# Adding own terms by accumulating DMAs in a two-branch adaLN block on one Trainium2 core

## The chip, the cores and the metric

The kernel runs on one core of one Trainium2 chip. The time is the device time of one execution in microseconds. TensorE (PE) multiplies matrices, VectorE (DVE), ScalarE (ACT) and GpSimd (POOL) work element by element on 128 partitions, SyncE (SP) issues DMAs. Each engine takes its instructions strictly in order and waits on semaphores for the others. A DMA issued by POOL can add to its destination instead of overwriting it.

## The reference

Four batches of 256 tokens by 256 channels go through two residual steps. Both start from the same two-sided weighted sum over the tokens, with `k = v = side` and decay `d` per batch and channel:

```python
ek = exp(min(k, 30)); ekv = ek * v
a = a * decay + ekv_t        # forward and reversed: nf, nb; the same for ek: df, db
euk = exp(min(u + k, 30))
num = nf + nb - ekv + euk * v
den = df + db - ek + euk
out = sigmoid(r) * num / max(den, 1e-8) * (0.8 + 0.2 * tf)
```

Branch 1 (weights w1, u1) feeds a gated recurrence: two 256 x 256 matmuls, `alpha = exp(-8 softplus(lambda) sigmoid(.))`, `beta = sqrt(1 - alpha^2 + 1e-6)`, and a linear scan over tokens; its result is added to x. Branch 2 (w2, u2), gated by the new x, feeds a mixture of experts: two shared experts for all tokens and the top 2 of 8 routed ones (hidden size 640). All is float32.

## The kernel before, in words

Channels lie on partitions, in two halves; a batch is a 128 x (2, 256) tile, and den and num stand side by side as four quarters (two of den, two of num). The work of a batch b is `front(b)` and `shared_units(b)`:

- `exps(b)`: POOL writes min(k, 30) (L432) and min(u + k, 30) (L437, four halves a batch) into `ek` and `own`, ACT takes the exponentials (L453, L460), DVE multiplies by v (L456, L464).
- `sums(b, n)` for branch n: a scan forward (L486, four quarters), its scaled last column (L492), and a scan backward over the forward sums (L499). The two-sided sum is (1 - d^2) times the backward scan (`rev`), plus the own term. Batch 0 (`BY_PE`) adds both on PE by matmuls with the identity and with a diagonal of 1 - d^2 (L513). Batches 1 to 3 add on DVE, two operations a branch (L521), each with the factor `both` = 1 - d^2, into the tile `fwd`.
- `most` takes the maximum with 1e-8 (batch 0 on ACT, L536; the others on DVE, L533). `quotient` takes 1/den as exp(-log) on ACT (L552 to L555), and three DVE operations make the gated product (L557/559, L560, L562).
- `gates` multiplies by x (L577), runs eight matmul steps on PE (L584), and then tanh, exponential, square and square root on ACT (L592 to L619) with two DVE steps (L598, L618). `recurrence` is L625, two scans (L628), the sum into x (L634), a tanh (L635) and the product `xt` (L637).
- `token_rows(b)` makes router scores and token-major rows on PE (L708, L715). `shared_units(b)` runs the shared experts: 40 matmul steps (L804), SiLU on ACT (L810), a product on DVE (L812), 20 matmul steps (L780). The 40 identity matmuls of `keep_warm` (L642) fill PE in batch 0.
- After the last front come `route`, `places` and `divide` (many small DVE operations), the scatter of token rows to DRAM (POOL, L974), loads of expert weights and rows (SP), and 18 slots of routed experts (L1065, L1081), each ended by an accumulating scatter into the output (L1095).

Natural logarithm, square root, SiLU and tanh need different ACT tables; a table load is L178. The DRAM rows are first blanked: POOL makes four empty rows (L683), and SP writes each out (L1318), which the scatter waits for.

The order is written out by hand: `ORDER` lists for each engine the numbers of the steps, which `Plan.run` emits in that order. Lengths and delays given with each step only merge the lists; they don't hold the chip to anything. A step that waits therefore holds all later steps of its engine.

Side and x of three batches are loaded at the start; batch 3 reuses the buffers of batch 0. The `own` and `ek` buffers alternate: batches 1 and 3 share one set, 0 and 2 the other.

Of the kernel before, what the change touches and what calls it, by code (L numbers as in the profile page):

```python
# [12 lines left out]
ALU = mybir.AluOpType  # L13
# [44 lines left out]

E30 = 10686474581524.463
# [8 lines left out]
        122 123 135 124 13 125 14 126 15 127 16 128 17 129 18 130 19 131 26 72 20 97 21 98 79 80 73 81 99 82 100 83  # L68
        75 84 85 101 132 86 133 87 88 118 134 119 136 120 137 150 197 102 138 77 103 145 104 173 201 174 105 169 163
        202 106 176 178 177 179 175 203 181 196 204 198 147 200 205 199 207 206 299 220 209 213 208 223 214 224 186  # L70
        225 215 238 305 311 192 317 210 217 325 149 212 216 211 219 218 251 392 226 380 233 379 257 261 381 262 391
        264 382 333 266 265 267 263 341 349 269 357 384 385 386 383 387 365 235 393 388 390 389 403 396 553 554 406
        555 407 280 408 274 421 237 397 474 398 480 492 394 416 418 395 400 399 401 434 402 557 409 486 559 558 556
        560 444 440 500 508 562 564 447 445 448 449 450 446 524 452 532 561 563 565 577 516 571 570 580 457 581 463
        572 582 617 584 618 566 765 567 540 620 771 621 574 568 420 569 597 573 576 575 619 583 622 623 603 624 631
        607 625 626 608 627 632 628 610 629 630 612 777 611 613 637 609 643 633 615 634 644 647 638 791 646 783 799
        670 664 639 641 642 673 674 640 676 677 675 678 645 679 683 680 684 681 682 807 696 697 689 698 685 699 700
        701 704 690 702 691 703 705 693 706 720 707 708 722 709 721 711 710 723 712 725 713 724 714 726 715 727 686
        815 728 694 716 729 730 731 717 695 718 692 719 732 736 823 852 831 858 737 870 738 739 878 864 886 894 902
        733 734 910 918 735  # L80
    """,
    "act": """
        71 24 22 25 23 74 78 76 115 116 117 144 121 171 172 155 164 156 167 166 165 168 161 162 170 195 180 148 146
        298 221 222 232 304 187 310 193 316 324 244 243 253 252 249 250 255 254 259 256 260 258 332 348 340 356 415
        268 234 364 236 378 419 404 405 375 275 417 479 374 485 473 491 281 427 426 436 435 432 433 438 437 439 442
        443 507 499 441 523 531 451 515 552 578 579 464 458 616 764 539 770 589 590 598 595 596 599 600 601 549 550
        602 605 606 604 776 790 614 782 798 806 672 665 822 814 671 851 830 857 840 863 869 841 877 885 901 893 909
        917 928 927
    """,
    "pe": """  # L90
        89 27 28 29 30 31 90 91 92 32 107 93 108 33 34 35 109 36 110 94 37 95 96 38 39 40 151 152 153 154 41 157 158
        111 42 159 43 44 160 45 46 47 48 49 112 50 51 52 53 54 113 55 56 57 58 114 59 60 61 62 63 64 65 66 290 292
        293 291 294 295 306 307 296 182 300 301 188 297 302 303 189 312 183 190 313 320 191 308 321 184 185 322 318
        319 323 309 314 315 239 240 241 242 245 246 247 352 248 353 326 336 344 345 328 327 337 354 338 346 355 335
        334 329 330 347 339 331 342 350 343 351 358 359 360 361 362 363 367 366 368 270 276 369 277 481 475 271 482
        272 469 371 373 487 483 278 484 488 370 273 470 372 476 477 279 471 467 489 478 490 472 422 423 424 428 429
        425 465 503 504 430 468 431 519 505 494 495 520 466 496 521 497 493 501 502 498 511 510 506 509 512 517 513
        527 522 528 529 530 525 533 518 526 514 535 536 534 537 766 459 453 460 454 767 768 461 455 462 772 456 760
        541 542 538 769 543 761 762 763 545 585 586 587 591 588 592 593 594 778 786 547 544 546 548 773 794 787 774
        788 779 795 775 789 758 756 757 784 759 796 780 792 781 797 785 635 793 636 802 803 804 800 801 805 660 666  # L100
        661 667 662 663 668 669 808 818 816 819 810 826 820 811 687 688 824 847 848 812 809 821 817 849 832 813 827
        825 850 833 835 828 829 853 834 836 859 860 861 838 854 873 855 856 865 866 874 881 837 882 862 843 867 868
        844 839 875 876 845 871 883 846 897 872 889 884 879 887 898 890 905 880 891 913 899 888 914 896 892 895 904
        903 915 900 906 907 912 908 920 911 916 919 921 922 924 926 923 925
    """,
    "pool": """
        67 68 69 70 142 143 139 140 227 141 288 230 228 231 410 411 413 229 284 286 412 282 414 658 659 657 652 648
        651 655 656 649 654 743 653 741 742 740 650
    """,
    "sp": """  # L110
        194 283 285 287 289 377 376 551 744 745 842 746 747 749 750 751 748 752 753 754 755 929
# [77 lines left out]
def adaln_attn_ffn(ctx: ExitStack, tc, xT, sideT, cond, par, wio, wr, wall, out):  # L189
# [11 lines left out]
    def fixed(name, *shape, dtype=F32):  # L201
        return const.tile([P, *shape], dtype, name=name)
# [72 lines left out]

    out_tf = fixed("out_tf", B)
# [80 lines left out]
    def tiny_step(emit, reads, writes):  # L357
        dve(2, emit, reads, writes, 11)

    def factors():  # L360
# [17 lines left out]
        tiny_step(lambda: nc.vector.reciprocal(onward, both), ["both"], ["onward"])  # L378
        tiny_step(
            lambda: nc.vector.scalar_tensor_tensor(onward, onward, -1.0, decays, ALU.mult, ALU.mult), ["decay", "onward"], ["onward"]  # L380
        )
        tiny_step(lambda: nc.vector.tensor_scalar(both, both, -1.0, None, ALU.mult), ["both"], ["both"])
        for n in (1, 2):
            for c in range(NC):
                act(
                    P, lambda n=n, c=c: nc.scalar.activation(
                        weigh[n][:, c, :], ident, AF.Copy, scale=both[:, n - 1, c, 0:1]
                    ),
                    ["both"], [("act", ACTS - n)], 11,
                )  # L390
        tiny_step(lambda: nc.vector.tensor_scalar(out_tf, tf, -0.1, -0.4, ALU.mult, ALU.add), ["tf"], ["out_tf"])

    def softplus():
# [9 lines left out]
        one(lambda: nc.vector.tensor_scalar(ser, s2, 1.0 / 17.0, None, ALU.mult), ["s2"], ["ser"])  # L403
        for k in (15, 13, 11, 9, 7, 5, 3):
            one(
                lambda k=k: nc.vector.scalar_tensor_tensor(ser, ser, 1.0 / k, s2, ALU.add, ALU.mult),
                ["ser", "s2"], ["ser"],
            )
# [8 lines left out]
    begun = []  # L417
# [7 lines left out]
    def exps(b):  # L425
# [7 lines left out]
        for n, j in ((1, U1), (2, U2)):  # L433
            d = own[n][k]
            for c in range(NC):
                pool(
                    lambda d=d, c=c, j=j: nc.gpsimd.tensor_scalar(  # L437
                        d[:, c, :], v[:, c, :], par_sb[:, j, c : c + 1], 30.0, ALU.add, ALU.min
                    ),
                    sv, [("own", n, k, 0)], r + 1, length=1450 if b == 0 else 1700,  # L440
                )
# [29 lines left out]
    def sums(b, n):  # L471
# [47 lines left out]
        for c in range(NC):  # L519
            dve(  # L520
                512, lambda c=c: nc.vector.scalar_tensor_tensor(  # L521
                    f[:, c::NC, 0:T], r[:, c::NC, 0:T], both[:, n - 1, c, b : b + 1], o[:, c::NC, :], ALU.mult, ALU.add
                ),
                [("rev", n, c), ("rev", n, NC + c), *halves("own", n, k), "both"], [("fwd", n, k, c), ("fwd", n, k, NC + c)], rank,
            )

    def most(b, n):

        k = b % 2
        den = fwd[n][k][:, 0:NC, 0:T]  # L530
        fs = [("fwd", n, k, h) for h in range(NC)]
        if (b, n) not in BY_PE:
            dve(256, lambda: nc.vector.tensor_scalar(den, den, DEN, None, ALU.max), fs, fs, 10 * b + 9)  # L533
            return
        q = bank_of(b, n)
        act(512, lambda: nc.scalar.activation(den, banks[q], AF.Relu, bias=less[:, 0:1]), [("bank", q)], fs, 10 * b + 10 + n)  # L536

    def quotient(b, n):
# [6 lines left out]
        ns = [("fwd", n, k, h) for h in range(NC, 2 * NC)]  # L545
        num, nkeys = f[:, NC:, :], ns
# [8 lines left out]
        act(512, lambda: nc.scalar.activation(y, y, AF.Exp, scale=-1.0), yk, yk, r, tables=(LOG,))  # L555
# [17 lines left out]
    def gates(b, q, qkeys):  # L573
# [4 lines left out]
        for which, dst, name in ((1, gate, "gate"), (0, xb, "xb")):  # L578
# [11 lines left out]
            for m in range(NC):  # L590
                act(
                    400, lambda m=m, which=which, dst=dst, pio=pio: nc.scalar.activation(  # L592
                        dst[:, m, :], pio[:, m, :], AF.Tanh, bias=half_b[:, which, m : m + 1], scale=0.5
                    ),
                    [("one", o), "half_b"], [(name, m)], r, tables=th,
                )
# [697 lines left out]
    def front(b):  # L1294
# [8 lines left out]
        if b + 1 < B:  # L1303
            exps(b + 1)
        gates(b, *q1)
        q2 = quotient(b, 2)
# [94 lines left out]
```

## Time and profile before

| | |
|---|---|
| median of three runs | 302.14 us (301.39 to 303.08) |
| the profiled execution's own time | 302.88 us |
| its span, first to last instruction | 300.7 us |
| busy in the span: PE, DVE, ACT, POOL | 280.6, 166.8, 125.2, 80.6 us |

The profile is one execution. A line of a group or timeline gives the source line, the engine, the operation, the tiles written and read, and how often; idle time before it is put down to what released it. "L804 PE" is the shared experts' first matmul. A matmul step in float32 shows as two records of the same line.

### The profile page before, as it was taken

To read this page: it belongs to the slowest core of one execution; us is meant where nothing else is said; L and a number is where in the kernel's file an instruction comes from. 1 tells how busy PE (TensorE), PEld (TensorE's weight loads), DVE (VectorE), ACT (ScalarE), POOL (GpSimd) and SP (SyncE) were. 2 spreads that over 40 slices of the span, in tenths; PEclk is the share of its full clock that TensorE was granted. 3 is DMA by queue.
4 is the path that set the end of the run, shared out by engine and by line. 5 is a ranking of instruction groups with operands and counts; after the bars stand their busy time and mean duration, and the time that the engine had idled before them with its cause. 6 is when DMAs were issued, how large, how long until landed. Compare 5 with 4: busy or idle time off the path is not lost. (4 is left out here: it accounts for less than half of the span.)

```text
span 300.7 us, 5206 instructions
## 1 busy us (share of the span) xinstructions
PE 280.6 (93%) x1902; PEld 247.4 (82%) x1902; DVE 166.8 (55%) x484; ACT 125.2 (42%) x250; POOL 80.6 (27%) x101
## 2 busy tenths in 40 slices
PE   7689899999999999969999999999999999999780
PEld 7579788888888888858888996899899999976770
DVE  4989999999999999860212152222322222242220
ACT  3397776997796696211212212212112111222100
POOL 6997031920000001756000002202242222124242
PEclk9799999999999999999999999999999999999995
DMA  6941000089992010269569999999269932881321
GB/s 204 442 179 35 1 3 0 0 302 353 352 348 89 0 35 2 98 216 425 183 227 430 427 415 416 408 396 401 49 170 349 326 108 35 282 280 21 39 31 22
DMA packets 22427, 60.88 MB, mean 202 GB/s; under 512 B 1920, under 2 KB 19200, under 8 KB 19840
## 3 DMA queue, kind: packets, MB, share of 16 engines
q1 hardware_dynamic: 18480, 55.02, 48.9%
q0 software_dynamic: 3360, 4.59, 8.1%
q10 hardware_dynamic: 560, 0.92, 0.9%
q8 instruction: 16, 0.26, 0.4%
q14 instruction: 11, 0.09, 0.1%
HBM read 44.60 MB, written 15.93 MB: 201 GB/s over the span
## 5 line engine op out<-in xcount | busy, mean ns | idle before, releaser
L804 PE MATMUL bank<-xt,shared 128*128 128x256 f32 x320 | 80.3, 382 | 0.8 <-DVE xt L637 0.8
L1065 PE MATMUL bank<-xg,late 128*128 128x128 f32 x640 | 75.1, 275 | 2.1 <-DVEq L1258 1.6
L1065 PEld LDWEIGHTS bank<-xg,late 128*128 128x128 f32 x640 | 73.3, 192 | 2.9 <-issue 2.3
L804 PEld LDWEIGHTS bank<-xt,shared 128*128 128x128 f32 x320 | 59.0, 190 | 9.2 <-DVE xt L637 1.3
L1072 DVE TENSOR_TENSOR act<-bank,act 128x256 f32<-128x256 f32 (+1 forms) x48 | 18.2, 380 | 70.6 <-ACT act L1071 69.2
L1095 POOL DMA_INDIRECT outT<-ys,to x16 | 24.8, 1551 | 114.5 <-DVE act L1072 40.9
L780 PE MATMUL acc<-shared,act 128*128 128x256 f32 x160 | 43.2, 382 | 2.3 <-DVE act L812 1.5
L1071 ACT ACTIVATE act<-bank 128x256 f32<-128x256 f32 (+1 forms) x48 | 16.7, 349 | 60.0 <-PE bank L1065 57.6
L1081 PE MATMUL acc<-late,act 128*128 128x256 f32 x160 | 37.7, 381 | 0.1
L780 PEld LDWEIGHTS acc<-shared,act 128*128 128x128 f32 x160 | 29.6, 190 | 7.2 <-DVE act L812 2.2
L178 ACT ACT_TABLE_LOAD x26 | 33.4, 1283 | 0.4
L974 POOL DMA_INDIRECT rows<-xtok,where x16 | 15.9, 992 | 64.1 <-DVE act L812 57.5
L1081 PEld LDWEIGHTS acc<-late,act 128*128 128x128 f32 x160 | 29.1, 190 | 4.6 <-issue 0.8
L437 POOL TENSOR_SCALAR late<-side,par_sb 128x256 f32<-128x256 f32 x16 | 26.4, 1650 | 10.9 <-DVE late L521 6.4
L810 ACT ACTIVATE act<-bank 128x256 f32<-128x256 f32 x40 | 13.9, 383 | 35.3 <-PE bank L804 35.0
L812 DVE TENSOR_TENSOR act<-bank,act 128x256 f32<-128x256 f32 x40 | 15.8, 415 | 19.7 <-ACT act L810 19.4
L486 DVE TENSOR_TENSOR_SCAN late<-decays,late 128x256 f32<-128x256 f32 x32 | 21.6, 704 | 0.0
L499 DVE TENSOR_TENSOR_SCAN late<-decays,late 128x257 f32<-128x257 f32 x32 | 21.1, 688 | 0.0
L1047 ACT COPY xg<-one 128x256 f32<-128x256 f32 x18 | 6.6, 374 | 33.6 <-PE one L1045 33.6
L584 PE MATMUL one<-late,wio_sb 128*128 128x256 f32 x64 | 15.7, 383 | 1.7 <-DVE late L577 1.7
L584 PEld LDWEIGHTS one<-late,wio_sb 128*128 128x128 f32 x64 | 11.6, 190 | 3.9 <-DVE late L577 1.7
L642 PEld LDWEIGHTS acc<-ident 128*128 128x128 f32 x80 | 11.9, 207 | 0.7
(224 smaller groups left out, 312.8 us busy)
## 6 DMA issues: line engine op xcount, KB each, us to landing
late<-in_wall SPq DMA_DIRECT2D x12, 1920.0 KB, 9.5
quad<-in_wall SPq DMA_DIRECT2D x6, 1920.0 KB, 11.2
rows<-quad SPq DMA_DIRECT2D x8, 1224.0 KB, 12.7
shared<-in_wall SPq DMA_DIRECT2D x2, 1920.0 KB, 9.0
xr<-rows SPq DMA_DIRECT2D x16, 136.0 KB, 7.9
side<-in_sideT SPq DMA_DIRECT2D x4, 256.0 KB, 4.6
outT<-base SPq DMA_DIRECT2D x4, 256.0 KB, 4.5
x<-in_xT SPq DMA_DIRECT2D x3, 256.0 KB, 9.6
```

Source lines behind the costliest of these rows:

```text
L178: line.append((free.get(engine, 0), len(line), lambda t=table: load_table(t)))
L437: lambda d=d, c=c, j=j: nc.gpsimd.tensor_scalar(d[:, c, :], v[:, c, :], par_sb[:, j, c : c + 1], 30.0, ALU.add, ALU.min),
L486: 0, lambda h=h: nc.vector.tensor_tensor_scan(f[:, h, 0:T], decay(h % NC, T), src[:, h, :], 0.0, ALU.mult, ALU.add),
L499: 0, lambda h=h: nc.vector.tensor_tensor_scan(r[:, h, 0 : T + 1][:, ::-1], decay(h % NC, T + 1), f[:, h, 0 : T + 1][:, ::-1], 0.0, ALU.mul ...
L584: 256, lambda m=m, k=k, which=which, pio=pio: nc.tensor.matmul(pio[:, m, :], wio_sb[:, which, k, bass.ts(m, P)], xc[:, k, :], start=(k == ...
L780: 256, lambda j=j: nc.tensor.matmul(acc[j], acts[a][:, bass.ts(j, P)], shared[s][:, GU + i * C : GU + (i + 1) * C], start=False, stop=((s, ...
L804: 256, lambda ps=ps, gu=gu, g=g, c=c, i=i: nc.tensor.matmul(ps[:, g, :], gu[:, g, c, bass.ts(i, P)], xt[k][:, c, :], start=(c == 0), stop= ...
L1065: nc.tensor.matmul(ps[:, g, i, :], gu[:, g, k, bass.ts(i0 + i, P)], self.xg[:, k, :], start=(k == 0), stop=(k == NC - 1),)
L1071: nc.scalar.activation(hid[:, 0:n, :], ps[:, 0, 0:n, :], AF.Silu)
L1072: nc.vector.tensor_tensor(hid[:, 0:n, :], ps[:, 1, 0:n, :], hid[:, 0:n, :], ALU.mult)
L1081: nc.tensor.matmul(self.py, self.acts[i], self.weights[:, GU + i * C : GU + (i + 1) * C], start=(i == 0), stop=(i == NI - 1),)
L1095: nc.gpsimd.indirect_dma_start(out=out[:, :], out_offset=bass.IndirectOffsetOnAxis(ap=self.to.bitcast(U32), axis=0), in_=ys, in_offset=Non ...
```

## The change

The diff, without the long number lists:

```diff
+ATANH = (0.12196954132, 0.10699280244, 0.14310103703, 0.19999355624, 0.33333339513)
...
     "pool": """
-        67 68 69 70 142 143 139 140 227 141 288 230 228 231 410 411 413 229 284 286 412 282 414 658 659 657 652 648
-        651 655 656 649 654 743 653 741 742 740 650
+        71 72 73 74 140 143 144 141 142 229 231 230 232 207 228 219 218 220 226 227 411 412 413 390 414 415 283 402
+        287 403 401 285 409 410 289 564 575 576 577 583 584 652 655 656 651 654 650 649 659 657 660 658 653 744 742
+        741 743
     """,
...
+    beside, limit, least = (fixed(name, 2, NC, B) for name in ("beside", "limit", "least"))
...
+        tiny_step(lambda: nc.vector.tensor_scalar(least, onward, -DEN, None, ALU.mult), ["onward"], ["least"])
...
+        def less_log():
+            act(16, lambda: nc.scalar.activation(limit, both, AF.Ln), ["both"], ["limit"], 11, tables=(LOG,))
+            us = par_sb[:, U1 : U2 + 1 : U2 - U1, :].unsqueeze(3).to_broadcast(shape)
+            tiny_step(lambda: nc.vector.tensor_tensor(beside, us, limit, ALU.subtract), ["limit"], ["beside"])
+            tiny_step(lambda: nc.vector.tensor_scalar(limit, limit, -1.0, 30.0, ALU.mult, ALU.add), ["limit"], ["limit"])
...
-        one(lambda: nc.vector.tensor_scalar(ser, s2, 1.0 / 17.0, None, ALU.mult), ["s2"], ["ser"])
-        for k in (15, 13, 11, 9, 7, 5, 3):
+        one(lambda: nc.vector.tensor_scalar(ser, s2, ATANH[0], None, ALU.mult), ["s2"], ["ser"])
+        for a in ATANH[1:]:
...
+                u, most_ = (beside[:, n - 1, c, b : b + 1], limit[:, n - 1, c, b : b + 1]) if b else (par_sb[:, j, c : c + 1], 30.0)
                 pool(
-                    lambda d=d, c=c, j=j: nc.gpsimd.tensor_scalar(
-                        d[:, c, :], v[:, c, :], par_sb[:, j, c : c + 1], 30.0, ALU.add, ALU.min
+                    lambda d=d, c=c, u=u, most_=most_: nc.gpsimd.tensor_scalar(
+                        d[:, c, :], v[:, c, :], u, most_, ALU.add, ALU.min
...
-        for c in range(NC):
-            dve(
-                512, lambda c=c: nc.vector.scalar_tensor_tensor(
-                    f[:, c::NC, 0:T], r[:, c::NC, 0:T], both[:, n - 1, c, b : b + 1], o[:, c::NC, :], ALU.mult, ALU.add
...
+        keys = halves("own", n, k)
+        pool(
+            lambda: nc.gpsimd.dma_start(o, r[:, :, 0:T], accum_op=ALU.add), keys + [("rev", n, h) for h in range(2 * NC)], keys,
+            rank - 1, length=1050, late=3600,
+        )
...
+        if (b, n) not in BY_PE:
+            den, key = own[n][k], [("own", n, k, 0)]
+            for c in range(NC):
+                pool(
+                    lambda c=c: nc.gpsimd.tensor_scalar(den[:, c, :], den[:, c, :], least[:, n - 1, c, b : b + 1], None, ALU.max),
...
-            dve(256, lambda: nc.vector.tensor_scalar(den, den, DEN, None, ALU.max), fs, fs, 10 * b + 9)
...
+        act(512, lambda: nc.scalar.activation(den, banks[q], AF.Relu, bias=less[:, 0:1]), [("bank", q)], fs, 10 * b + 10 + n, tables=(LOG,))
...
+        if (b, n) not in BY_PE:
+            f = own[n][k]
+            den, ds, ns = f[:, 0:NC, :], [("own", n, k, 0)], [("own", n, k, 1)]
...
-                    [("one", o), "half_b"], [(name, m)], r, tables=th,
+                    [("one", o), "half_b"], [(name, m)], r, tables=th, after=[once[0, 2]],
```

In batches 1 to 3 num and den are now both divided by 1 - d^2. The own term gets its factor by subtracting log(1 - d^2) from the exponent (`beside`, and `limit` in place of 30), and one DMA a branch, issued by POOL, adds `rev` (128 x 1024 elements, 512 KB) onto `own` in SBUF. The maximum, with 1e-8 / (1 - d^2), is taken on POOL in two halves, and the quotient then works in `own`. The softplus series has four terms in place of seven. Batch 0 keeps its matmuls; its relu is bound to the logarithm's ACT table.

All five orders are new. Decoded, POOL runs: batch 0's and 1's minima, batch 2's four own minima, add(1, branch 1), batch 2's ek minimum, max(1,1) half 0, add(1,2), max(1,1) half 1, max(1,2) twice, three minima of batch 3, add(2,1), batch 3's last two minima, blank 0, max(2,1) half 0, blank 2, max(2,1) half 1, add(2,2), blank 1, max(2,2) twice, blank 3, add(3,1), add(3,2), four maxima, then the scatters of batches 0 to 2 and of batch 3. SP loads x of batch 3 ahead of the clears, and batch 2's output leaves after the first loads of rows and weights in place of before.

DVE in batch 0 up to the product `xc` of `gates` has, among the scans, the branch 2 backward scan of one quarter moved behind the first quotient step. In batch 1 it runs, from batch 0's `xt` on: one forward scan, one small step, the own product and the four backward scans of branch 1; then four forward scans, own product and four backward scans of branch 2, four expert products, four larger steps of batch 2 and three small ones; and only then the three quotient steps and `xc`. PE has 28 + 7 shared-expert steps of batch 0 ahead of batch 1's gate matmuls, where it had 20 + 2.

## The prediction

> **What bounds the kernel now.** I read the page's busy shares first, then PE's timeline around batch 0, PE's busy time over the shared experts, then DVE, ACT and POOL in batch 0 and 1, then the DMAs. The page and PE's timeline:
>
> ```profile
> PE 280.6 (93%) x1902; PEld 247.4 (82%) x1902; DVE 166.8 (55%) x484; ACT 125.2 (42%) x250; POOL 80.6 (27%) x101
> ...
> PE   7689899999999999969999999999999999999780
> ...
> DVE  4989999999999999860212152222322222242220
> ...
> 33.67 0.66 PE L791 MATMUL acc<-ident,x 128*128 128x128 f32 x4
> 35.12 2.43 PE L804 MATMUL bank<-xt,shared 128*128 128x256 f32 x10 [0.80 <-DVE xt L637]
> ...
> 131.00 0.70 PE L780 MATMUL acc<-shared,act 128*128 128x256 f32 x2 [0.88 <-DVE off_q L935]
> ...
> 134.88 0.70 PE L780 MATMUL acc<-shared,act 128*128 128x256 f32 x2 [1.46 <-DVE act L812]
> ```
>
> PE's shared experts start when batch 0's xt (L637) exists. Their phase, to the first routed rows, in the table of windows:
>
> ```profile
> 35.12:160.90 125.78, 123.02 (x596) 106.31 (x597) 100.76 (x272) 75.35 (x133) 28.24 (x28) 1.00 0.49 168
> ```
>
> PE works 123.02 of 125.78 us at full granted clock (the column of 1.00), so 2.76 us are idle, most of it while DVE divides the tokens at 130 to 135. The change touches none of this work. So although DVE is full from 7 to 112 us, its time is worth something in two places only: ahead of 35.12, and where PE waits. After 160.9 the slots run as before (PE's tenths stay at 9), and I let them move as a block; so does the tail.
>
> **Batch 0.** DVE and ACT timelines:
>
> ```profile
> 15.41 0.69 ACT L536 ACTIVATE late<-bank,less 128x512 f32<-128x512 f32 x1 [2.67 <-PE bank L513]
> 16.12 1.28 ACT L178 ACT_TABLE_LOAD   x1
> 17.41 0.72 ACT L552 ACTIVATE late<-late,less 128x512 f32<-128x512 f32 x1
> 18.17 0.63 ACT L555 ACTIVATE late<-late 128x512 f32<-128x512 f32 x1
> ...
> 18.83 1.11 DVE L557 SCALAR_TENSOR_TENSOR late<-late,late 128x512 f32<-128x512 f32 x1 [1.09 <-ACT late L555]
> ```
>
> The relu bound to the log table moves its 1.28 us load ahead of the relu, into the 2.67 us that ACT waits there. The new small logarithm adds two loads, one before it, one back for the tanh of x: 2.6 us, in ACT's waits of 2.30 us (before L386) and 1.03 (before the second L460) and the remaining 1.4 here; without that cover they would cost up to 2.6 on the same chain. DVE reaches L557 with one backward scan fewer (0.62 paced) and three softplus steps fewer, against three tiny new ones (each 0.1 to 0.2, equal): at about 16.6 from 17.74. The relu is ready between 14.6 and 15.9 (the first if PE's five dummy steps, now ahead of its first own term, close the 2.34 us gap before it; the second if they run slowly as at 11 to 13 us), so the quotient starts at 16.75 to 18.05 where it started at 18.83. Gain 0.8 to 2.1; I take 1.6, nearer the early end because the idle gap goes. From there both lists are equally long and ACT's chain from gate tanh to square root (24.34 to 30.85) keeps its length: L804 starts at 33.5 in place of 35.12. **Term: -1.6.**
>
> **The additions.** Gone from DVE: twelve L521 and six L533, added on POOL: six DMAs and twelve maxima. Rows:
>
> ```profile
> L521 DVE SCALAR_TENSOR_TENSOR late<-late,both,late 128x512 f32<-128x512 f32 x12 | 8.6, 742 | 0.1
> L533 DVE TENSOR_SCALAR late<-late 128x512 f32<-128x512 f32 x6 | 2.5, 411 | 0.0
> L437 POOL TENSOR_SCALAR late<-side,par_sb 128x256 f32<-128x256 f32 x16 | 26.4, 1650 | 10.9 <-DVE late L521 6.4 <-DVE late L464 2.0 <-DMA side<-in_sideT 1.4
> ...
> side<-in_sideT SPq DMA_DIRECT2D x1, 256.0 KB, 2.8
> ```
>
> That is 11.1 us off DVE, worth nothing by itself. What counts is the way from the last backward scan to the logarithm: before 2 x 0.66 + 0.33 = 1.7 us; now a DMA and two maxima of 1.65.
>
> No row shows this DMA: 512 KB, packets of 1 KB, SBUF onto SBUF. From below: the side load in a quiet window has the same packets and 256 KB: 2.8 us to landing, 0.81 of them engine time (shares 0.73, 0.85 and 0.04 of three half-microseconds). With twice the data 3.6, and POOL's issue of 0.98 (L974) for SP's 0.54: 4.05. From above: the 128-row accumulate into DRAM at 290.15 takes 1.54 of issue and lands after 3.77, with 1.19 of engine time; four times the data gives 7.35. I take 4.65, near the lower end, since its destination is SBUF as the side load's is. The plan charges 1.05 + 3.6 too; that is no measurement, though its 1280 ns for a scatter is the trace's spacing (121.05 to 122.36).
> The Trainium skill, page "DMA: Bandwidth & Descriptors", section "Anatomy of one DMA", fits 2.0 us plus bytes by 436 GB/s, 3.2 us here; its fit is for plain transfers. By it batch 1 below would have about 2.5 us more to spare.
>
> **Batch 1**, from xt of batch 0 (DVE end 33.4): six scans or products and a small step, 3.8, so the first DMA issues at 37 and lands at 41.7; maximum half 0 to 43.3; only then can POOL issue the second DMA (to 44.4); half 1 to 46.0; log and exp 1.2 and a copy; quotient 47.6, where DVE's own list arrives at 46.5; four steps of 0.6 to 0.74: xc at 50.3. PE comes there at 33.5 + 35 steps of 0.432 + 1.7 = 50.4. No wait. The second DMA lands at 48.0, maxima to 51.3, log and exp to 52.5, table 1.28; gate tanhs to square root 6.1; then 5.2 to xt at 65.1 (before: 63.8). PE arrives at its router matmuls at 65.3: before 64.34, less 1.6, plus five or six steps of batch 0 now ahead. So 0.2 to 0.3 us are spare, and each us more per DMA costs about 1.8 here, because two stand in a row on POOL.
>
> **Batches 2 and 3** meet the clears. They saturate the DMA engines:
>
> ```profile
> 86.00:87.00 1.00, 1.00 (x6) 0.89 (x5) 0.94 (x2) 0.86 (x3) 0.00 (x0) 1.00 1.13 348
> ...
> rows<-quad SPq DMA_DIRECT2D x8, 1224.0 KB, 12.7
> ```
>
> Blank 0 now waits on POOL behind batch 3's minima, which need batch 1's second quotient (60): clears from about 63.5 to 92. Batch 2's second DMA (issued about 68) and both of batch 3 (86, 88) fall in. One 1 KB packet of each of 32 per engine waiting for one clear packet (1088 bytes at 348 GB/s, 16 engines: 0.05) adds 1.6; the accumulate at 203.10 that lands after 9.65 us beside weight loads, where the quiet one took 3.8, bounds it from above at 5.9. I take 1.6, as the clears' packets are small. The same walk then has xt of batch 2 at 93 with PE there at 92.5, and batch 3's xc at 99 with PE at 98.2: waits of 0.5 and 0.8. Scatter needs the clears by about 108; they end near 95.
>
> **Division.** Routing of batches 0 to 2 now ends before batch 3's recurrence, and only four scatters stand behind batch 3's places (six before), 1.28 each: rows load some 8 us earlier, hidden, because PE reaches the slots only at 159. Moving batch 2's output behind the loads and batch 3's x ahead of the clears is free: neither has a reader nearby. Two further products are put behind some 45 small DVE steps (about 8 us), with 20 PE steps (8.7) to cover them; I allow 0.5 there and 0.5 at the counts. The 1.8 us that DVE stood at 131.3 until something remote may return; with it, 1.5 more.
>
> POOL's maxima also hold DVE up: a scan (L486) that began at 42.96, beside POOL's minimum of 42.57, took 1.10, the others about 0.70. At 0.1 to 0.4 each, 1.2 to 4.8 us of the 11.1 come back, off PE's path.
> The Trainium skill, "SBUF — State Buffer", section "Who interferes with whom", speaks against the change: a GpSimd operation that reads SBUF and a DVE operation with two SBUF inputs exclude each other for a whole instruction. By it twelve maxima cost DVE up to 20 us, which would turn the gain into a loss; no row here shows a hold that long.
>
> **Sum.** -1.6 (start) - 2.76 (old waits) + 0.5 + 0.8 + 0.5 + 0.5 = -2.1. The profiled execution's own 302.88 becomes 300.8. It lies 0.74 above the median; from 302.14: 300.0, range of this case 298.3 to 301.2.
>
> **Rivals.**
> 1. *Slower: the accumulating DMA takes more than about 5.3 us.* At x above 4.65, batch 1 loses 1.8x - 0.3, batches 2 and 3 x each; at x = 0.63 the 2.1 are gone, at 7.35 it is 4.6 + 5.4 - 2.1: 310. For it: the accumulate row's 1.19 us for 128 KB. Against: that is DRAM. I put it at 303.7 to 310, centre 305.5; chance 0.32.
> 2. *A wash:* the clears cost 2.3 to 3 rather than 1.6 on each of two DMAs (+1.4 to 2.8; at the upper bound of 5.9 it would be +8.6, inside case 1's range): 301.5 to 302.8. Chance 0.22.
> 3. *All waits go:* DMA at 4.05, clears not felt, start at 33.0: 33.0 + 123.0 in place of 160.9, -4.9: 297.3. Chance 0.08.
> The forecast keeps 0.38.
>
> 0.5% (1.5 us) is about what a measurement tells from no change: faster means below 300.6. The forecast's case lies below it with three quarters, plus case 3 and a little of case 2: 0.40. Same: the rest of the forecast, most of case 2 and the foot of case 1: 0.25. Slower 0.35. The range leaves out case 3's end and the last third of case 1: 297.6 to 307.0.
>
> **What would show it.** PE's first L804 near 33.5; a relu directly followed by its logarithm; DMAs of late onto late landing in about 4.7 us in batch 1 and 6.3 in batches 2 and 3; PE's waits at L584 and L708 of batches 1 to 3 under 1 us each; first L1045 near 158.8. I am wrong if PE waits for several us at L584 or L708 (DMA or maxima too slow), or if L804 starts no earlier.

## The result and the profile after

The changed kernel takes 324.56 us (median of four runs, 323.64 to 326.33); the kernel before, on the same chip, takes 302.54 (301.39 to 303.08). The ratio is 1.074 with an interval of 1.068 to 1.080. The forecast was 300.0 us with a range of 297.6 to 307.0: slower where a small gain was forecast, and outside the range. The profiled execution took 324.15 us, with a span of 322.5.

From the page of the changed kernel, the busy shares, and PE's busy tenths and granted clock in 40 slices of 8 us each:

```profile
PE 284.3 (88%) x1902; PEld 250.4 (78%) x1902; DVE 159.0 (49%) x466; ACT 127.8 (40%) x253; POOL 106.5 (33%) x119
...
PE   7789998999599499999991299999999999999791
...
PEclk9999999999899899999998589999999999999997
```

DVE has lost 7.8 us of work, as the change meant, and POOL has gained 26. PE does the same 1902 matmuls. What is new are three dips in its row (5 and 4 near 85 and 110 us, 1 and 2 near 175), with a lower clock at each. Next, the idle times of PE over 0.3 us from the start of the shared experts to the first routed slot, in its timeline (start, duration, and in brackets the idle time before and what ended it):

```profile
33.61 0.70 PE L825 MATMUL bank<-xt,shared 128*128 128x256 f32 x2 [0.36 <-DVE xt L658]
...
51.70 3.69 PE L605 MATMUL one<-late,wio_sb 128*128 128x256 f32 x16 [1.38 <-DVE scores L740]
...
86.27 2.07 PE L825 MATMUL bank<-xt,shared 128*128 128x256 f32 x4 [3.54 <-DVE act L833]
109.46 5.38 PE L605 MATMUL one<-late,wio_sb 128*128 128x256 f32 x16 [5.05 <-DVE late L598]
...
169.83 0.60 PE L1066 MATMUL one<-ident,xr 128*128 128x128 f32 x4
183.69 8.68 PE L1086 MATMUL bank<-xg,late 128*128 128x128 f32 x56 [13.26 <-ACT xg L1068]
```

In the kernel before, where PE started at 35.12 (in the prediction's first fence), the other two marks were these:

```profile
160.90 0.60 PE L1045 MATMUL one<-ident,xr 128*128 128x128 f32 x4
161.80 6.52 PE L1065 MATMUL bank<-xg,late 128*128 128x128 f32 x56 [0.30 <-ACT xg L1047]
```

Read as a budget: PE starts 1.5 us earlier (33.61 against 35.12), reaches the first row transposes 8.9 us later (169.83 against 160.90), and starts the first routed slot 21.9 us later (183.69 against 161.80). So 13 of the 22 us are one wait, and 10.4 lie in the shared phase, of which the start gives back 1.5. The table of windows (length; busy time of PE, PEld, DVE, ACT, POOL; then granted clock, DMA share, GB/s) splits these further. The changed kernel, shared phase and then the stretch around the big wait:

```profile
33.61:169.83 136.22, 125.95 (x596) 108.69 (x597) 93.62 (x254) 74.96 (x132) 50.25 (x48) 0.97 0.66 200
169.83:192.50 22.67, 9.41 (x63) 9.15 (x62) 1.14 (x3) 2.33 (x8) 0.00 (x0) 0.70 0.49 195
```

The kernel before, the stretch that answers to the second:

```profile
160.90:168.40 7.50, 7.20 (x63) 6.93 (x62) 1.14 (x3) 2.01 (x7) 0.00 (x0) 1.00 1.00 427
```

The shared phase has 10.27 us of PE idle (136.22 - 125.95), where there were 2.76, and the same 596 records take 125.95 us where they took 123.02. In the second stretch the same 63 records take 9.41 us in place of 7.20, at a granted clock of 0.70 in place of 1.00. So each long wait costs twice: by itself, and by a slower restart. The Trainium skill, page "TensorE: Matmul & The Clock Gate", section "What's actually happening", says that the clock falls to half after about 3.4 us without work; the waits of 3.54, 5.05 and 13.26 us here are all above that, and the clock falls to 0.50 behind each of them. In the kernel before it also stood at 0.50, from 12 to 14 us, behind a wait of only 2.34 us (8.3 to 10.6), so the length of one wait is not the whole rule here.

**The 13 us.** ACT's timeline of the changed kernel:

```profile
182.72 0.65 ACT L842 COPY base<-acc 128x256 f32<-128x256 f32 x2 [16.77 <-DMA outT<-base]
183.25 0.67 ACT L1068 COPY xg<-one 128x256 f32<-128x256 f32 x2
```

Its SP timeline (start and duration of the issues; the last line joins those of batch 2's and batch 3's outputs, which lie 25.5 us apart, so its 25.88 is no transfer time):

```profile
153.71 0.35 SPq L1024 DMA_DIRECT2D late<-in_wall  x1
154.58 2.39 SPq L1024 DMA_DIRECT2D quad<-in_wall  x3
157.48 0.33 SPq L1024 DMA_DIRECT2D late<-in_wall  x1
157.91 25.88 SPq L844 DMA_DIRECT2D outT<-base  x2
```

And its list of waits (us in total, times, longest):

```profile
ACT base L842 <- DMA outT<-base: 16.8, 1, 16.8
```

Batch 2's output is issued on SP at 157.91, right behind five loads of 1920 KB. At the 425 to 434 GB/s of the page's two slices from 161 to 177 us those 9.8 MB alone need 23 us, and the 256 KB of output land behind them, at about 182.7. ACT's copy of batch 3's result into `base` overwrites what that transfer reads, and waits for it 16.77 us. Behind the copy stands the copy of the first routed rows (`xg`, L1068), and behind that all of the routed experts on PE.

**The 10 us.** POOL's timeline of the changed kernel: issue of an addition (L536), then the first maximum (L547) that waits for its landing. The first pair is batch 1's, the others those of batches 2 and 3:

```profile
37.81 1.52 POOL L536 DMA_DIRECT2D late<-late  x1 [5.59 <-DVE late L514]
...
43.52 0.92 POOL L547 TENSOR_SCALAR late<-late,least 128x256 f32<-128x256 f32 x1 [2.07 <-DMA late<-late]
...
71.12 1.31 POOL L536 DMA_DIRECT2D late<-late  x1 [3.20 <-ACT late L576]
...
79.89 2.70 POOL L547 TENSOR_SCALAR late<-late,least 128x256 f32<-128x256 f32 x2 [6.91 <-DMA late<-late]
...
91.97 1.30 POOL L536 DMA_DIRECT2D late<-late  x1 [8.91 <-ACT late L638]
94.40 1.28 POOL L536 DMA_DIRECT2D late<-late  x1 [1.13 <-ACT late L640]
102.89 1.81 POOL L547 TENSOR_SCALAR late<-late,least 128x256 f32<-128x256 f32 x2 [7.21 <-DMA late<-late]
106.31 2.17 POOL L547 TENSOR_SCALAR late<-late,least 128x256 f32<-128x256 f32 x2 [1.61 <-DMA late<-late]
```

From issue to maximum it is 5.7 us for the quiet one, and 8.8, 10.9 and 11.9 beside the clears (eight of 1224 KB, until about 99 us; behind them the last two additions still move data until 105). What stands behind these, in DVE's timeline:

```profile
79.82 1.51 DVE L514 TENSOR_TENSOR_SCAN late<-decays,late 128x257 f32<-128x257 f32 x2 [4.01 <-DMA late<-late]
...
106.12 0.69 DVE L580 TENSOR_TENSOR late<-late,late 128x512 f32<-128x512 f32 x1 [6.46 <-ACT late L576]
```

And in ACT's:

```profile
82.62 0.63 ACT L575 ACTIVATE late<-late 128x512 f32<-128x512 f32 x1 [6.92 <-POOL late L547]
...
85.22 0.38 ACT L831 ACTIVATE act<-bank 128x256 f32<-128x256 f32 x1
```

The logarithm of batch 2 (L575) waits 6.92 us for the maxima, and the SiLU of the shared experts (L831) stands behind it, an exponential and a table load: that is PE's wait of 3.54 at 86.27. The quotient of batch 3 waits 6.46 in the same way: PE's 5.05 at 109.46. The first line of DVE shows a second path: batch 3's backward scan writes the tile `rev` that batch 2's addition is still reading.

**What went as forecast.** ACT's timeline in batch 0:

```profile
15.36 0.69 ACT L554 ACTIVATE late<-bank,less 128x512 f32<-128x512 f32 x1 [1.83 <-PE bank L528]
16.08 0.72 ACT L573 ACTIVATE late<-late,less 128x512 f32<-128x512 f32 x1
```

DVE's:

```profile
17.49 0.69 DVE L578 SCALAR_TENSOR_TENSOR late<-late,late 128x512 f32<-128x512 f32 x1 [0.28 <-ACT late L576]
```

The logarithm follows the relu with no table load between them, the quotient starts at 17.49 in place of 18.83, and the start of PE at 33.61 is the 33.5 of the prediction.

### The profile page after: what moved, and what is told of

Its sections match the earlier page's. It is cut to its first block, busy times and chain, and to the rows that moved or that the text cites. A ratio compares the mean times of both kernels' runs of the same rounds, so it can differ in the third digit from the quotient of the medians.

```text
span 322.5 us, 5242 instructions
## 1 busy us (share of the span) xinstructions
PE 284.3 (88%) x1902; PEld 250.4 (78%) x1902; DVE 159.0 (49%) x466; ACT 127.8 (40%) x253; POOL 106.5 (33%) x119
## 4 chain that ended last, share of the span: by engine, by line
PE 50%; DMA 21%; ACT 10%; DVE 7%; issue 6%; POOL 3%; POOLq 1%; ACTq 0%; DVEq 0%
PE bank L1086 20%; PE acc L1102 9%; PE bank L825 8%; DMA late<-late 8%; DMA outT<-base 8%; PE acc L801 5%; DMA outT<-ys,to 4%; ACT L180 3%; POOL late L547 2%; PE one L605 2%; PE bank L528 2%; PE bank L1183 1%; DMA outT<-sums,to 1%; DVE late L501 1%; DVE late L514 1%
## 5 line engine op out<-in xcount | busy, mean ns | idle before, releaser
L1086 PE MATMUL bank<-xg,late 128*128 128x128 f32 x640 | 77.1, 280 | 15.0 <-ACT xg L1068 13.3
L1086 PEld LDWEIGHTS bank<-xg,late 128*128 128x128 f32 x640 | 75.4, 197 | 15.7 <-ACT xg L1068 13.5
L825 PEld LDWEIGHTS bank<-xt,shared 128*128 128x128 f32 x320 | 59.7, 193 | 12.7 <-DVE act L833 3.9
L801 PE MATMUL acc<-shared,act 128*128 128x256 f32 x160 | 42.3, 383 | 0.3 <-DVE act L833 0.3
L831 ACT ACTIVATE act<-bank 128x256 f32<-128x256 f32 x40 | 13.7, 384 | 33.5 <-PE bank L825 29.2
L452 POOL TENSOR_SCALAR late<-side,beside,limit 128x256 f32<-128x256 f32 x12 | 24.1, 2018 | 1.6 <-DVE limit L394 1.2
L605 PE MATMUL one<-late,wio_sb 128*128 128x256 f32 x64 | 17.0, 415 | 7.8 <-DVE late L598 6.5
L995 POOL DMA_INDIRECT rows<-xtok,where x16 | 17.1, 1068 | 14.8 <-DVE where L885 9.8
L605 PEld LDWEIGHTS one<-late,wio_sb 128*128 128x128 f32 x64 | 12.9, 208 | 11.0 <-ACT late L575 5.4
L547 POOL TENSOR_SCALAR late<-late,least 128x256 f32<-128x256 f32 x12 | 13.8, 1155 | 21.2 <-DMA late<-late 21.2
L1068 ACT COPY xg<-one 128x256 f32<-128x256 f32 x18 | 6.6, 375 | 33.4 <-PE one L1066 33.4
```

What stands on the lines that cost most here:

```text
L452: lambda d=d, c=c, u=u, most_=most_: nc.gpsimd.tensor_scalar(d[:, c, :], v[:, c, :], u, most_, ALU.add, ALU.min),
L547: lambda c=c: nc.gpsimd.tensor_scalar(den[:, c, :], den[:, c, :], least[:, n - 1, c, b : b + 1], None, ALU.max),
L605: 256, lambda m=m, k=k, which=which, pio=pio: nc.tensor.matmul(pio[:, m, :], wio_sb[:, which, k, bass.ts(m, P)], xc[:, k, :], start=(k == ...
L801: 256, lambda j=j: nc.tensor.matmul(acc[j], acts[a][:, bass.ts(j, P)], shared[s][:, GU + i * C : GU + (i + 1) * C], start=False, stop=((s, ...
L825: 256, lambda ps=ps, gu=gu, g=g, c=c, i=i: nc.tensor.matmul(ps[:, g, :], gu[:, g, c, bass.ts(i, P)], xt[k][:, c, :], start=(c == 0), stop= ...
L1086: nc.tensor.matmul(ps[:, g, i, :], gu[:, g, k, bass.ts(i0 + i, P)], self.xg[:, k, :], start=(k == 0), stop=(k == NC - 1),)
```

## The experiments

Two theories for the loss: A, the place of batch 2's output on SP; B, the additions of batches 2 and 3 beside the clears. Each was undone alone, both together, and A was put into the kernel before alone. Ratios are to the kernel before on the same chip, which took 300.90 us for these four kernels, 301.71 for batch 0 alone and the first one with halves, and 300.99 for the other two.

**Batch 2's output back in its place.**

```diff
 SP's order, decoded
-W0 W1 rows0 rows1 W2 rows2 rows3 rows4 part0 .. part3, output of batch 2, ...
+W0 W1, output of batch 2, rows0 rows1 W2 rows2 rows3 rows4 part0 .. part3, ...
```

> The changed kernel with one step moved on SP: batch 2's output leaves after the first two weight loads, as before the change, and not behind five rows, a weight load and four quarter loads. Theory A (this order costs the large gap: batch 2's output waits in SP's DMA ring behind some 10 MB of weights, batch 3's copies into the same tile base wait for it on ACT, and the first slots' tile xg stands behind them on ACT): ACT's wait of 16.8 us at L842 and PE's of 13.3 us at L1086 go, and with them some 2 us of matmuls at a reduced granted clock; 307 to 311 us against 324.6. Rival (the weights themselves arrive late, whatever stands before them, and another wait takes its place): still above 318, with PE idle at about 170 to 180 for a weight or row DMA.

Measured: 311.39 us, ratio to the kernel before 1.037 (1.034 to 1.040). PE's timeline:

```profile
172.51 6.52 PE L1090 MATMUL bank<-xg,late 128*128 128x128 f32 x56 [0.62 <-ACT xg L1072]
```

The wait of 13.26 us is 0.62, and the first slot is back at 6.52 us, as in the kernel before. The waits of 3.56 us near 87 and of 4.83 at batch 3's gates stay. Theory A holds for its part, with a time just above the 311 expected.

**The clears spread, ahead of the additions.**

```diff
 POOL's order, decoded
-... ownmin(3), blank 0, max(2,1) half 0, blank 2, max(2,1) half 1, add(2,2), blank 1, max(2,2) twice, blank 3, ...
+ekmin(1), blank 0, blank 1, ..., max(1,2) half 1, blank 2, ..., add(2,2), max(2,2) twice, blank 3, ...
 SP's order: clears 0 and 1 ahead of the load of batch 3's side
-            length=700, after=[added])
+            length=700)
```

> The changed kernel with the clears of the DRAM rows moved out of the accumulating DMAs' way: blanks 0 and 1 on POOL right after batch 1's ek minimum (some 14 us), their clears on SP ahead of the loads of batch 3; blank 2 after batch 1's last maximum; blank 3 stays after batch 2's. Batch 2's output stays late. Theory B (the clears' traffic lengthens the additions of batches 2 and 3 from 5.5 to 9 to 12 us, and PE's waits of 3.5 us at L825 and 5.1 us at L605 come from it): all six additions land in 5.5 to 6.5 us, these two waits shrink to under 1.5 us each, the shared experts end some 8 us earlier, 313 to 318 us. Rival (the additions are slow in themselves, or wait for each other): landing above 8 us as now, time above 321.

Measured: 314.46 us, ratio 1.047 (1.043 to 1.051). PE's timeline:

```profile
83.66 1.13 PE L829 MATMUL bank<-xt,shared 128*128 128x256 f32 x4 [0.20 <-DVE act L837]
96.19 0.61 PE L733 MATMUL one<-wr_sb,xt 128*128 128x8 f32 x4 [1.04 <-DVE xt L662]
174.29 9.23 PE L1090 MATMUL bank<-xg,late 128*128 128x128 f32 x56 [13.30 <-ACT xg L1072]
```

The wait of 3.54 is 0.20 and that of 5.05 at batch 3's gates is gone; a wait of 1.04 at a router is new. From issue to maximum the three additions that took 8.8 to 11.9 us now take 5.5 to 6.4 (the first was issued at 71.78, its maximum came at 77.30). The wait for `base` stays at 13.30, although PE is there 9 us earlier: SP also issues the loads and the output 8 us earlier (149.99 in place of 157.91), and the output again lands some 23 us after its issue. Theory B holds for its part.

**Both.** The two edits together.

> Both moves together in the changed kernel. Theories A and B: 15 and 8 us of the 22 go, which leaves 300 to 304 us, about the kernel before. If the rest of the change has a cost of its own that neither move touches (DVE held up by POOL's maxima, slower matmuls): 305 to 309.

Measured: 300.42 us, ratio 1.0015 (0.998 to 1.005): the whole loss is gone, and no gain is left. PE's timeline:

```profile
34.00 0.70 PE L829 MATMUL bank<-xt,shared 128*128 128x256 f32 x2 [0.36 <-DVE xt L662]
52.43 3.69 PE L609 MATMUL one<-late,wio_sb 128*128 128x256 f32 x16 [1.71 <-DVE scores L744]
...
95.81 0.61 PE L733 MATMUL one<-wr_sb,xt 128*128 128x8 f32 x4 [1.03 <-DVE xt L662]
```

The window of its shared phase:

```profile
34.00:160.34 126.34, 123.27 (x599) 106.65 (x600) 93.33 (x254) 75.04 (x133) 48.53 (x44) 1.00 0.53 152
```

The start is 1.1 us earlier than before, and 3.07 us of idle time (126.34 - 123.27) stand in the place of 2.76. The division's two waits are gone; batch 1's gates (1.71) and a router (1.03) have taken their place.

**The kernel before with only the output moved.**

```diff
 SP's order of the kernel before, decoded
-... W1, output of batch 2, rows0 ... part3, ...
+... W1, rows0 ... part3, output of batch 2, ...
```

> The kernel before with that one step moved the other way: batch 2's output goes behind the first rows, weight 2 and the four quarter loads on SP, all else unchanged. Theory A: batch 3's copies into base wait on ACT until about 178 to 182, PE stands 12 to 18 us before the first slots; 315 to 322 us against 302.5. Rival (harmless, as the prediction had it: nothing near reads or writes the tile): 301 to 304.

Measured: 321.26 us, ratio 1.068 (1.061 to 1.075). ACT's timeline:

```profile
180.61 0.65 ACT L824 COPY base<-acc 128x256 f32<-128x256 f32 x2 [24.17 <-DMA outT<-base]
```

SP's:

```profile
157.90 23.79 SPq L826 DMA_DIRECT2D outT<-base  x2
```

PE's:

```profile
181.59 9.07 PE L1068 MATMUL bank<-xg,late 128*128 128x128 f32 x56 [22.11 <-ACT xg L1050]
```

One step, moved on SP past the loads of rows and five loads of weights, makes the kernel before 20 us slower. It costs more here than in the changed kernel since PE stands at the first slot 11 us earlier (159.5 against 170.4) while the output is issued at the same 157.9. The lateness that the additions cause hides little of the loss: with the clears spread PE stood there at 161.0, but SP issued the output at 149.99, and the wait was 13.30 as before; from there to both edits it is 14.0 us. The two edits bring 3.7 and 2.7% alone and 7.2% together, which is their sum to within the intervals.

Then, why is nothing left of the 1.1 us at the start?

**Batch 0 alone**, in the kernel before.

```diff
+            if b == 0:
+                q2 = quotient(b, 2)
...
-        act(512, lambda: nc.scalar.activation(den, banks[q], AF.Relu, bias=less[:, 0:1]), [("bank", q)], fs, 10 * b + 10 + n)
+        act(512, lambda: nc.scalar.activation(den, banks[q], AF.Relu, bias=less[:, 0:1]), [("bank", q)], fs, 10 * b + 10 + n, tables=(LOG,))
...
 softplus with four terms; orders of the changed kernel up to batch 0's xt, then of the kernel before
```

> The kernel before with the batch 0 part alone: the shorter softplus, the relu bound to the logarithm's table, the gate tanhs after batch 0's second reciprocal, and the changed kernel's orders up to batch 0's xt; from there the orders of before, no accumulating DMA, no maxima on POOL, own terms and clears as before. Theory (the gain of batch 0 is real, and nothing after it gives it back, because batches 1 to 3 keep their short way from scan to logarithm): L804 starts at 33.6 to 34.2 in place of 35.1, no new waits of PE at L584 or at the router matmuls, 299.3 to 300.0 against 300.9 for the kernel before on this chip. Then the accumulating DMAs give back all that batch 0 gains, since both moves together gave 300.4. Rival (the start is earlier, but batch 1's xt is not, so PE waits there): no change, 300.5 to 301.3.

Measured: 301.43 us, ratio 0.998 (0.995 to 1.001). The theory missed, and the rival came nearer in its number, though not in its place: batch 1's gates waited only 0.51 us. PE started its shared experts at 34.37; its timeline at the division, of an execution that took 303.77 us:

```profile
130.57 0.70 PE L785 MATMUL acc<-shared,act 128*128 128x256 f32 x2 [0.99 <-DVE off_q L940]
134.94 0.84 PE L785 MATMUL acc<-shared,act 128*128 128x256 f32 x2 [1.94 <-DVE act L817]
```

PE starts 0.75 us earlier, and waits 2.93 us at the division where it waited 2.34 in the kernel before. DVE's timeline there:

```profile
131.25 0.17 DVE L963 SCALAR_TENSOR_TENSOR part_row<-slots,off_q 128x8 int32<-128x8 f32 x1 [1.01 <-DVE off_q L940]
133.38 0.22 DVE L940 TENSOR_REDUCE number_q<-sq 128x8 f32<-128x64 f32 x1 [1.82 <-remote]
```

So it isn't the length of DVE's list that PE waits for there: DVE itself stands idle for 1.01 and 1.82 us between small steps of its own, and in the kernel before for 0.35 and 1.80 at the same steps. In the run above with only the output moved, DVE went through the same steps without a stop, and PE had no wait at the division. What stops DVE the traces don't show ("remote"), and there is one trace of each kernel; so what takes back the earlier start in the other executions stays open.

**And with the late order.** The kernel of batch 0 alone, with the changed kernel's orders for PE, ACT and DVE from batch 3's xt on, where the changed kernel has no wait at the division.

```diff
 orders of PE, ACT and DVE, decoded: of the changed kernel from batch 3's xt, tanh and router on
```

> The kernel before with the change's batch 0 (order up to batch 0's xt, relu's log table, shorter softplus), and from batch 3's xt on the changed kernel's order for PE, ACT and DVE; additions and maxima of batches 1 to 3, clears and the place of batch 2's output as in the kernel before. Theory: the earlier start at batch 0 (0.7 us in the run with batch 0 alone) was lost because PE waited 0.99 and 1.94 us for DVE in the division at 130 to 135 us (0.88 and 1.46 in the kernel before), and the changed kernel's order has no wait there (none in the run with both steps put back); so 2 to 2.9 us come off: 298.6 to 299.6 us, both waits under 0.3 us. Rival: the weights and rows end the phase whatever PE does, or DVE is late there anyway: the waits move to other matmuls or to the first routed slot, and the time stays at 301 to 302 us.

Measured: 302.16 us, ratio 1.0055 (1.003 to 1.008). PE's timeline:

```profile
124.37 0.37 PE L841 MATMUL one<-upto,ones 128*128 128x24 f32 x2 [2.34 <-DVE total L768]
```

The rival held: PE started at 34.25, and the waits moved from the division to the counts ahead of it, with 0.99 us more at 118.98 and 0.53 at 133.36. With its additions on DVE this kernel has DVE busy for 32.28 of the 35 us from 90 to 125 (28.92 in the last kernel below). That points to DVE's load ahead of the counts as what eats the earlier start here, where DVE has no stop at the division; it wasn't varied by itself.

**What an addition is made of.** The kernel with both edits, with plain copies in place of accumulating ones. It leaves the own terms out, so tokens are routed otherwise and its total tells nothing.

```diff
-            lambda: nc.gpsimd.dma_start(o, r[:, :, 0:T], accum_op=ALU.add), keys + ...
+            lambda: nc.gpsimd.dma_start(o, r[:, :, 0:T]), keys + ...
```

> Both moves, with plain copies in place of the accumulating DMAs: it leaves the own terms out of batches 1 to 3's sums, and so routes other tokens to other experts. It measures what adding costs. If the bound from below was right (packets of 1 KB into SBUF move as fast as in the quiet side load, 0.81 us per 256 KB): landing in 3.9 to 4.3 us, data time 1.6 us at about 320 GB/s. If the read-back of the destination is not what slows it: landing 5.3 to 5.6 as now, at 172 GB/s.

Measured: 307.39 us, a single time. PE's waits at batch 1's gates and at the router are 0.56 and 0.36 us here, in place of 1.71 and 1.03, so these two hang on how long the additions take. The rates of batch 1's first transfer, 512 KB, in 40 slices: first the changed kernel from 39 to 43 us (0.1 us each), then the plain copy from 39 to 42 (0.075 us each):

```profile
GB/s 0 0 0 0 0 0 0 0 10 82 164 174 174 184 164 184 174 164 184 174 184 164 164 184 164 174 164 174 174 195 164 164 174 174 184 164 205 164 154 103
```

```profile
GB/s 0 0 0 0 0 437 382 437 273 328 437 218 492 273 328 437 218 492 273 382 328 273 492 273 219 0 0 0 0 0 0 0 0 0 0 0 0 0 0 0
```

The accumulating transfer runs at about 172 GB/s for 3.2 us, the plain one at about 350 for 1.5. The plain one moves 4 KB packets where the accumulating one moves 1 KB, so that accumulating itself or the smaller packets halve the rate; which of the two wasn't separated.

**Additions in halves.** On top of both edits. As each sum's den is wanted first, batches 1 and 2 got two transfers of 256 KB a sum, den first, batch 1's two maxima of a sum one after the other, and batch 2's ek minimum went ahead of the first addition.

```diff
+        if b < 3:
+            for half in range(2):
+                part, key = slice(half * NC, half * NC + NC), [("own", n, k, half)]
+                pool(
+                    lambda part=part: nc.gpsimd.dma_start(o[:, part, :], r[:, part, 0:T], accum_op=ALU.add),
...
+            return
```

> Both moves (batch 2's output early, clears spread), and in batches 1 and 2 each addition as two DMAs of 256 KB, the denominators first, so that the maxima need not wait for the numerators; batch 1's maxima stand together ahead of its second additions, and batch 2's ek minimum ahead of the first. Theory (the remaining cost is the way from the last scan to the logarithm; of the 5.5 us of an addition about 3.1 are data): the first half lands in about 4 us, batch 1's logarithm starts 2 us earlier than 47.5, PE's waits of 1.7 us at the gate matmuls and 1.0 at the router matmuls go, 298 to 299.5. Rival (POOL's two issues of 1.3 us in a row eat the gain, or PE waits elsewhere): 300 to 301.

Measured: 304.5 us, ratio 1.009 (1.006 to 1.012); a miss. Batch 1's wait went, and a new one came:

```profile
124.08 0.49 PE L869 MATMUL one<-upto,ones 128*128 128x24 f32 x2 [3.88 <-DVE total L796]
```

DVE stood idle from 115.46 to 120.96 there, before batch 3's first scores, although PE's matmuls for these had run by 117. What held it isn't seen in the trace and stays open.

**Only batch 1 in halves.** The same with `if b == 1`, and batch 2 as in the changed kernel.

```diff
-        if b < 3:
+        if b == 1:
```

> The changed kernel with clears spread and batch 2's output after W1, and batch 1's two additions alone sent as two DMAs of 256 KB each, denominators first, each sum's two maxima together; batches 2 and 3 as in the changed kernel. Theory: the wait of 1.71 us at batch 1's gates is the landing of the 512 KB addition and goes (under 0.5 us), the router's wait of 1.03 us stays, and the wait at the counts that came with the split of batches 1 and 2 (3.88 us) came from batch 2: 298.7 to 299.8 us. Rival: the two DMAs of batch 1 alone bring the wait at the counts back: 301.5 to 304 us.

Measured: 298.41 us, ratio 0.992 (0.989 to 0.995): less than both kernels, and 0.8% below the one before. PE's timeline, in an execution that took 301.37 us, with the clock at 0.90 in the first 33 us:

```profile
96.72 0.61 PE L741 MATMUL one<-wr_sb,xt 128*128 128x8 f32 x4 [1.04 <-DVE xt L670]
```

The window of its shared phase:

```profile
36.51:161.17 124.66, 123.28 (x599) 106.54 (x600) 92.91 (x254) 75.07 (x133) 52.02 (x46) 1.00 0.53 151
```

No wait is left at batch 1's gates, the router's 1.04 stays, and the idle time of the phase is 1.38 us (124.66 - 123.28), where both edits alone had 3.07 and the kernel before 2.76. The long wait at the counts hasn't come. That points to what was done to batch 2 (the halves, or its ek minimum ahead), but as what held DVE there isn't seen, it isn't shown.

## Why the prediction was wrong

- **The step that failed** is in the part on the division: "Moving batch 2's output behind the loads and batch 3's x ahead of the clears is free: neither has a reader nearby." The output has no reader, but it is one itself: it reads `base`, and the next writer of `base` is ACT's copy of batch 3, ahead of the first routed rows on ACT. The number was in reach: five loads of 1920 KB stand right ahead of it on SP. It cost 13.3 us of waiting and 2 us of clock in the changed kernel, and 20 us by itself in the kernel before. None of the rivals held it. The Trainium skill, page "DMA: Bandwidth & Descriptors", section "Queues, rings and completion order", says that each DMA engine takes what one issuing engine gave it in order; the landing 25 us after the issue agrees.
- **"I take 1.6, as the clears' packets are small"** was mis-sized. Beside the clears an addition took 8.8 to 11.9 us, 3.1 to 6.2 more than the 5.7 of the quiet one. The bound of 5.9 from the accumulate at 203.10 was the nearer row. The sum had waits of 0.5 and 0.8 us; PE waited 3.54 and 5.05, and the slower clock after them added 2.9 us over the phase. That the running addition also holds the next writer of `rev` wasn't seen.
- **The addition, "I take 4.65"**, took 5.7 from issue to maximum, with 1.3 to 1.5 of issue where 0.98 was set. That is past the 5.3 where rival 1 was to decide. By its rule (1.8x - 0.3 in batch 1, x in each of the other two, x = 1.05) the cost is 3.7 us, which would leave the kernel 1.6 us slower than before, since the forecast's gain was 2.1. With both edits the trace has 2.9 us of new waits (0.20, 1.71 and 1.03), and the time is that of the kernel before to within 0.5% (300.42 against 300.90). So rival 1 was right in kind, and its price 1 to 2 us too high. But the 22 us aren't its work: with both edits the additions are as long and the loss is gone. The page "DMA: Bandwidth & Descriptors" of the skill, section "Anatomy of one DMA", gave 3.2 us; the plain copy came to 3.7 (issue at 37.78, maximum at 41.49), the accumulating one to 5.7.
- **"Term: -1.6"** for batch 0 was right in its mechanism: the logarithm starts at 16.08 in place of 17.41, behind a relu that is no earlier (15.36, 15.41), and PE at 33.61, or at 33.40 to 34.37 in seven other kernels that have it. How much of the 1.5 us is the change's own is open. In these eight traces the granted clock from 11 to 15 us was 1.00, in the kernel before 0.57; the eighth other kernel, with 0.59 there, started at 36.51, later than the 35.12 of the kernel before. Wrong was what the term is worth. The prediction counted it in full, but alone it came to -0.2% (interval -0.5 to +0.1%); in its trace PE then waits 0.6 us longer at the division, where DVE stands idle.
- **Batch 1**, "xc at 50.3" and "No wait": PE came at 50.3, and xc was late by 1.38 (1.71 with both edits), by the longer addition. Taking its landing in halves removed that.
- **The division**, "I allow 0.5 there and 0.5 at the counts": no wait at either place. Right in direction; the run with the late order shows that the order alone doesn't do it, and the old waits at the division also went in the kernel before with only the output moved, where DVE didn't stop. The prediction had named that stop ("The 1.8 us that DVE stood at 131.3").
- **"POOL's maxima also hold DVE up"**, 1.2 to 4.8 us: small, and within that range at most. A forward scan took 702 ns on average where it had taken 704, a backward one 693 where it had been 688; products of the own terms (L471) took 775 where they had taken 702 (four of them), the recurrence's scans 710 where 676 (eight). DVE's busy time fell by 7.8 us where rows of 11.1 were taken away, so at most 3.3 us came back, overlapping records among them. The up to 20 us that the skill's page "SBUF — State Buffer", section "Who interferes with whom", would allow didn't come.
- **The rows of what would show it** worked: "I am wrong if PE waits for several us at L584 or L708" names the 5.05. For the largest wait, at the first slot, no row had been named, since the slots were let "move as a block".

## What to carry to other kernels

A store that is moved on a queue is to be walked like any other step: what lies ahead of it on that queue, in bytes, by the measured rate, against the next writer of the tile that it reads. Work taken off an engine that isn't the bound pays only if the way that replaces it is no longer from the last producer to the first reader; here 11 us of DVE became a chain through POOL and the DMA queues, and its worth hung on what else was in these queues at that time. And undoing two suspects one by one and both together shows whether their losses add up; putting one of them alone into the old kernel shows that it needs nothing else of the change.

## What was not expected of the hardware

- An accumulating transfer from SBUF onto SBUF moves 512 KB at about 172 GB/s (1 KB packets), a plain one at about 350 (4 KB packets); issue on POOL takes 1.3 to 1.5 us, the plain one 0.75 to 1.03.
- Beside transfers that fill the DMA engines (1224 KB clears), the same addition took 8.8 to 11.9 us in place of 5.7.
- After 13.3 and 22.1 us without matmuls, the 56 matmuls of the first slot took 8.68 and 9.07 us in place of 6.52.
- Twelve maxima of about 1.15 us on POOL left DVE's 64 scans of the sums as they were, to within 5 ns on average.
